# L1's self layers: transposing the attention weights head by head, and moving them in 4 KB pieces

## The chip, the cores and the metric

The kernel runs on one core of a Trainium2 chip, as one program. The metric is the time of one execution on the device in microseconds (us). The core has five engines with a queue of instructions each: TensorE (PE, matmuls; PEld is its loading of weights), VectorE (DVE), ScalarE (ACT), GpSimd (POOL) and SyncE (SP). Each runs its queue in order, and waits on semaphores for the others. DMAs are issued from SP's and POOL's queues here and run beside the engines.

## The reference

Four residual attention blocks follow one another on x (4 sequences of 1024 tokens, 256 channels, float32): L0 (self and cross attention, 16 heads, and a feed-forward part), L1 (three layers of 4 heads of 64 channels), L2 and L3 (16 heads, against a context of 77 tokens). The change is in L1, whose first layer attends to the context and whose second and third attend to their own tokens:

```python
Q = jax.nn.relu(q @ Wq + bq); K = jax.nn.relu(k @ Wk + bk); V = jax.nn.relu(v @ Wv + bv)
scores = jnp.einsum('hbqd,hbkd->hbqk', Qh, Kh) / jnp.sqrt(jnp.float32(dh))
scores = jnp.where(key_mask[None, :, None, :] == 0.0, NEG, scores)
attn = jax.nn.softmax(scores, axis=-1) * query_mask[None, :, :, None]
out = _layer_norm(jnp.einsum('hbqk,hbkd->hbqd', attn, Vh) + q, gamma, beta)
enc = jax.nn.leaky_relu(out @ Wff[i] + bff[i], negative_slope=0.2) + out
```

## The kernel before

All of x stays on the chip. A pipe (class Pipe) goes through the layers and, in each, through the four sequences. An item is one layer of one sequence. Its attention is cut into units; between the units the pipe's pump hands out steps of other work (projections of the next item, layer norm and output matmul of the one before) by costs that are written beside them. Only PE's order is the order of the text (manual_schedule); the queues of the other engines are ordered when the program is built, from what is ready, with the earlier instruction in the text first. `issue_after(ins)` adds that all instructions of a block on the engine of `ins` are queued behind `ins`; it adds no wait for its end.

In the self layers (class Self4) an item has 16 units: two pairs p of heads by eight tiles t of 128 query tokens. A unit does the following.

- Scores (L1262): for both heads h of the pair, PE multiplies 128 queries with all 1024 keys into a PSUM buffer `ss` of its own, [128, 1024]. There are two such buffers, so the next unit's scores of head h must wait until this unit's exponential of head h has read them.
- Maxima (L1273): VectorE reduces each `ss` to the negative maxima `nm`.
- Exponentials (L1279): ACT writes exp(ss + nm) into the buffer PR, and adds up the rows (`accum_out`). It permutes the columns as it writes: key number (k, c, i) of 8 x 4 x 32 goes to (c, k, i).
- The weights must be turned so that keys lie on the partitions. That is done by blocks: VectorE transposes each 32 x 32 block in place (L1291), and DMAs carry the blocks to other partitions of a buffer PT (L1298). A PR buffer holds a pair of units, t even and t odd; there are two, as of PT. The DMAs of a pair go out together: 16 of 128 KB, from 32 partitions (a) to 32 partitions (c).
- Weighted sums (L1334): PE multiplies the values V with PT, in two halves.
- `normal` (L1352 to L1364) turns the sums back, divides by the row sums and adds them to x.

The text puts these parts in different units. `scores` is called in unit u. `turned_by_blocks` is called in unit u + 1, behind the scores of that unit: it has the transpose of unit u, and, where t is odd, the pair's DMAs, SP and POOL taking turns with a. The halves of the weighted sums follow in units u + 3 and u + 4.

The lengths of the DMA pieces come from the layouts: PR is [128, 2 (t), 2 (h), 4 x 256], and a DMA takes 256 columns of each t and h, so its 32 partitions have four pieces of 1 KB each.

In the same queues stand, among others: on VectorE the statistics and scaling of the layer norm (L1536, L1583, L1586), its reciprocals and `normal`; on ACT all copies out of PSUM (L1512), the projections' Relu (L1233, L1194); on POOL the power of the variance (L1385); on SP the weights of the next layer (L1028, L1033), the bias rows cut into three parts (`thirds`, L2061) and the mask row of the keys (L1179). In the cross layer, L1501 and L1505 copy turned weights to a buffer PTc, on VectorE and ACT by turns.

## Time and profile before

| | us |
|---|---|
| median of 3 runs (2395.11 to 2406.44) | 2396.89 |
| the profiled execution, its own time | 2396.79 |
| its span, first to last instruction | 2394.9 |
| first to last unit of the self layers, from the span's start | 948 to 1880 |
| PE busy in the span | 2204.3 |
| VectorE busy | 1582.6 |
| ACT busy | 930.2 |
| POOL busy | 380.4 |

The page of the profile gives busy times, a row of 40 slices for each engine (a digit is the busy share in tenths), and groups of instructions: line, engine, operation, written and read buffers with their shapes, the number of instructions, then their busy time in us, the mean duration in ns, and the idle time of the engine just before them, with what ended most of it. The timeline gives start, duration, engine and line of single instructions, and in brackets an idle time before them with its end's cause. The granted clock is the share of its full clock that TensorE was given. A view of one buffer gives durations as least, median and greatest in ns.

### The profile page before, as it was taken

To read this page: it belongs to the slowest core of one execution; us is meant where nothing else is said; L and a number is where in the kernel's file an instruction comes from. 1 tells how busy PE (TensorE), PEld (TensorE's weight loads), DVE (VectorE), ACT (ScalarE), POOL (GpSimd) and SP (SyncE) were. 2 spreads that over 40 slices of the span, in tenths; PEclk is the share of its full clock that TensorE was granted. 3 is DMA by queue.
4 is the path that set the end of the run, shared out by engine and by line. 5 is a ranking of instruction groups with operands and counts; after the bars stand their busy time and mean duration, and the time that the engine had idled before them with its cause. 6 is when DMAs were issued, how large, how long until landed. Compare 5 with 4: busy or idle time off the path is not lost. (4 is left out here: it accounts for less than half of the span.)

```text
span 2394.9 us, 31195 instructions
## 1 busy us (share of the span) xinstructions
PE 2204.3 (92%) x11035; PEld 1204.8 (50%) x11035; DVE 1582.6 (66%) x3167; ACT 930.2 (39%) x1828; POOL 380.4 (16%) x648
## 2 busy tenths in 40 slices
PE   6899999999898979999999899999999899999996
PEld 3565446566577655545454445454545344444442
DVE  6665553534424565888888788888888656656765
ACT  2222332222232355545454454444444234434333
POOL 2000000000000000333333233333333100000000
PEclk8999989989998998999999999999999899999988
DMA  5000010000000000667776577766787400000000
GB/s 147 1 3 14 5 36 1 1 3 5 12 1 7 1 5 1 146 147 152 151 156 144 123 151 157 151 142 141 148 163 143 97 5 1 5 1 1 27 18 28
DMA packets 148677, 158.01 MB, mean 66 GB/s; under 512 B 51432, under 2 KB 130849, under 8 KB 148513
## 3 DMA queue, kind: packets, MB, share of 16 engines
q1 hardware_dynamic: 122161, 85.63, 17.2%
q0 software_dynamic: 25296, 69.24, 13.1%
q8 instruction: 91, 1.49, 0.3%
q10 hardware_dynamic: 1056, 1.05, 0.1%
q14 instruction: 73, 0.60, 0.1%
HBM read 17.41 MB, written 4.19 MB: 9 GB/s over the span
## 5 line engine op out<-in xcount | busy, mean ns | idle before, releaser
L1279 ACT ACTIVATE PR<-ss,nm 128x1024 f32<-128x1024 f32 x256 | 284.7, 1114 | 366.2 <-DVE nm L1273 290.2
L1291 DVE STREAM_TRANSPOSE PR<-PR 128x2048 f32<-128x2048 f32 x128 | 295.8, 2311 | 128.9 <-ACT PR L1279 114.3
L1298 POOL DMA_DIRECT2D PT<-PR x512 | 279.6, 554 | 577.7 <-PE ss L1262 236.7
L1262 PE MATMUL ss<-QK 64*128 64x512 f32 x1024 | 324.8, 628 | 28.8 <-ACT PR L1279 28.5
L1273 DVE TENSOR_REDUCE nm<-ss 128x1 f32<-128x1024 f32 x256 | 299.6, 1210 | 13.8 <-PE ss L1262 13.8
L377 ACT ACTIVATE PT<-pb 77x1024 f32<-77x1024 f32 x192 | 185.4, 1015 | 193.2 <-PE pb L373 193.2
L1334 PE MATMUL po<-PT,V 128*64 128x256 f32 x2048 | 251.1, 387 | 5.1 <-DMA PT<-PR 5.1
L281 DVE TENSOR_REDUCE mx<-pa 128x4 f32<-128x308 f32 x384 | 161.4, 470 | 83.7 <-PE pa L276 82.5
L1262 PEld LDWEIGHTS ss<-QK 64*128 64x128 f32 x1024 | 113.3, 187 | 176.8 <-ACT PR L1279 99.7
L1334 PEld LDWEIGHTS po<-PT,V 128*64 128x64 f32 x2048 | 136.6, 137 | 108.4 <-issue 51.1
L276 PE MATMUL pa<-KA,QT 64*128 64x308 f32 x768 | 169.1, 486 | 14.0 <-DVE mx L281 12.8
L1545 POOL TENSOR_TENSOR pw<-va,minus_half 128x4 f32<-128x4 f32 (+1 forms) x28 | 38.8, 1384 | 714.5 <-DVE va L1543 542.0
L386 PE MATMUL po<-PT,Vc 77*32 77x512 f32 x768 | 140.4, 639 | 7.6 <-ACT PT L377 7.0
L276 PEld LDWEIGHTS pa<-KA,QT 64*128 64x128 f32 x768 | 84.3, 193 | 99.1 <-issue 37.0
L604 PE MATMUL pp<-hF,w 128*128 128x256 f32 x512 | 116.9, 382 | 0.0
L367 PE MATMUL pb<-QT,KA 32*77 32x512 f32 x768 | 114.1, 665 | 0.0
L619 PE MATMUL pp<-w,hid 128*128 128x256 f32 x512 | 113.7, 379 | 0.0
L619 PEld LDWEIGHTS pp<-w,hid 128*128 128x128 f32 x512 | 97.0, 190 | 16.5 <-issue 2.2
L604 PEld LDWEIGHTS pp<-hF,w 128*128 128x128 f32 x512 | 95.6, 190 | 18.2 <-issue 6.0
L266 PE MATMUL pp<-hT,wq 128*128 128x512 f32 x192 | 98.0, 646 | 5.5 <-ACT hT L1507 5.0
L1536 DVE BATCH_NORM_STATS2 st<-x 128x6 f32<-128x256 f32 x256 | 97.7, 403 | 3.2 <-DMA x<-in_x 2.3
L1405 PE MATMUL pp<-wo,hE 128*128 128x256 f32 x384 | 96.4, 393 | 1.6 <-ACT hE L1512 1.6
(256 smaller groups left out, 3079.5 us busy)
## 6 DMA issues: line engine op xcount, KB each, us to landing
PT<-PR SPq DMA_DIRECT2D x512, 128.0 KB
PT<-PR POOLq DMA_DIRECT2D x512, 128.0 KB, 4.9
x<-in_x SPq DMA_DIRECT2D x4, 1024.0 KB
out<-x SPq DMA_DIRECT2D x8, 512.0 KB
w<-in_ff_w SPq DMA_DIRECT2D x2, 1024.0 KB
gb<-in_norms POOLq DMA_DIRECT2D x5, 256.0 KB, 6.6
wk<-in_l_wk SPq DMA_DIRECT2D x10, 128.0 KB
wv<-in_l_wv SPq DMA_DIRECT2D x5, 256.0 KB
```

The costliest lines, as they stand in the source:

```text
L276: nc.tensor.matmul(pas[i], self.qt[rows, e, ts(t, P)], self.ka[rows, e, :, :], start=True, stop=True)
L281: nc.vector.tensor_reduce(out, pas[i].rearrange("p (j s) k -> p j s k", s=2), AX.X, ALU.max, negate=True)
L377: nc.scalar.activation(pt[:, 2 * i : 2 * i + 2, :], pbs[i][:SC], AF.Exp, scale=self.l.scale)
L386: nc.tensor.matmul(po[ts(j, h.slot), :], l.v[:, self.b, col : col + h.vw], pt[:, j, :], start=True, stop=True)
L604: nc.tensor.matmul(pp[:, i, :], self.w1[:, cc, ts(f + i, P)], s["hT"][:, cc, ts(q, 2 * P)], start=cc == 0, stop=cc == NC - 1)
L619: nc.tensor.matmul(pp[:, u, :], s["a"][:, f, ts(u, P)], self.w2[:, f, :], start=f == 0, stop=f == NF - 1)
L1262: nc.tensor.matmul(ss[h][:, k, :], self.qk[p][rows, 0, ts(t, P)], self.qk[p][rows, 1, ts(k, 512)], start=True, stop=True,)
L1273: nc.vector.tensor_reduce(self.nm[:, t, at], s2, AX.X, ALU.max, negate=True)
L1279: nc.scalar.activation(out, s2, AF.Exp, bias=self.nm[:, t, at], accum_out=self.sums[:, t, at])
L1291: nc.vector.transpose(part, part)
L1298: (nc.sync, nc.gpsimd)[a % 2].dma_start(out=pt[ts(c, 32), :, :, a].rearrange("p t h k j -> p (t h) (k j)"), in_=pr[ts(a, 32), :, :, ts(c, ...
L1334: nc.tensor.matmul(po[64 * h : 64 * h + 64], self.v[:, k, 64 * (2 * p + h) : 64 * (2 * p + h) + 64], pts[:, :, h, :, k, :] if net.blocks e ...
```

## The change

The transposes move from `turned_by_blocks` into `scores`, into the unit whose weights they turn, and there are two of them, one for each head; both are queued behind the maxima of that unit's second head. `turned_by_blocks` is left with the DMAs and is called for odd t alone. PR is laid out as [128, 4 (c), 2 (t), 2 (h), 256], so that what one DMA takes from a partition is one piece of 4 KB; the exponential writes four pieces of 256 columns, 4 KB apart, where it wrote 1024 in a row, and a head's transpose works on such four pieces. PT has its dimension a ahead of t and h to match, so the written piece is of 4 KB too. SP issues the DMAs of a = 0, 1 and 2, POOL those of a = 3: twelve and four of a pair's sixteen. The weighted matmul reads the same 256 columns, in runs of 32, at other strides.

```diff
@@ scores @@
-            self.pr = net.tile("E", [P, 2, 2, S], name="PR")
+            self.pr = net.tile("E", [P, 4, 2, 2, S // 4], name="PR")
         for h in range(2):
             at = slice(2 * p + h, 2 * p + h + 1)
             s2 = ss[h].rearrange("p k n -> p (k n)")
-            nc.vector.tensor_reduce(self.nm[:, t, at], s2, AX.X, ALU.max, negate=True)
+            reduced = nc.vector.tensor_reduce(self.nm[:, t, at], s2, AX.X, ALU.max, negate=True)
             if net.blocks:
-                out = self.pr[:, t % 2, h, :].rearrange("p (c k i) -> p k c i", c=4, i=32)
+                out = self.pr[:, :, t % 2, h, :].rearrange("p c (k i) -> p k c i", i=32)
                 s2 = s2.rearrange("p (k c i) -> p k c i", c=4, i=32)
             else:
                 out = pr[:, h, :]
             nc.scalar.activation(out, s2, AF.Exp, bias=self.nm[:, t, at], accum_out=self.sums[:, t, at])
         if net.blocks:
-            net.pipe.later("next", 1, lambda pr=self.pr: self.turned_by_blocks(p, t, pr))
+            with net.tc.issue_after(reduced.ins):
+                for h in range(2):
+                    part = self.pr[:, :, t % 2, h, :]
+                    nc.vector.transpose(part, part)
+            if t % 2:
+                net.pipe.later("next", 1, lambda pr=self.pr: self.turned_by_blocks(p, t, pr))
@@ turned_by_blocks @@
-        part = pr[:, t % 2].rearrange("p h s -> p (h s)")
-        nc.vector.transpose(part, part)
-        if t % 2 == 0:
-            return
-
-        pt = net.tile("B", [P, 2, 2, 4, NT, 32], name="PT")
+        pt = net.tile("B", [P, 4, 2, 2, NT, 32], name="PT")
         for c in range(4):
             for a in range(4):
-                (nc.sync, nc.gpsimd)[a % 2].dma_start(
-                    out=pt[ts(c, 32), :, :, a].rearrange("p t h k j -> p (t h) (k j)"),
-                    in_=pr[ts(a, 32), :, :, ts(c, 256)].rearrange("p t h n -> p (t h) n"),
+                (nc.gpsimd if a == 3 else nc.sync).dma_start(
+                    out=pt[ts(c, 32), a].rearrange("p t h k j -> p (t h k j)"),
+                    in_=pr[ts(a, 32), c].rearrange("p t h n -> p (t h n)"),
                 )
@@ weighted @@
-                    pts[:, :, h, :, k, :] if net.blocks else pts[:, :, h, k, :], start=k == 0, stop=k == NT - 1,
+                    pts[:, :, :, h, k, :].rearrange("p a t j -> p t a j") if net.blocks else pts[:, :, h, k, :], start=k == 0, stop=k == NT - 1,
```

## The prediction

> **What bounds the kernel now.** The page comes first. The change touches only the self-attention of L1's second and third layer, where the lines L1262 to L1334 run; they fill the span from 948 to 1880 us.

> ```profile
> PE 2204.3 (92%) x11035; PEld 1204.8 (50%) x11035; DVE 1582.6 (66%) x3167; ACT 930.2 (39%) x1828; POOL 380.4 (16%) x648
> DVE  6665553534424565888888788888888656656765
> ...
> L1279 ACT ACTIVATE PR<-ss,nm 128x1024 f32<-128x1024 f32 x256 | 284.7, 1114 | 366.2 <-DVE nm L1273 290.2
> L1291 DVE STREAM_TRANSPOSE PR<-PR 128x2048 f32<-128x2048 f32 x128 | 295.8, 2311 | 128.9 <-ACT PR L1279 114.3
> ...
> L1273 DVE TENSOR_REDUCE nm<-ss 128x1 f32<-128x1024 f32 x256 | 299.6, 1210 | 13.8 <-PE ss L1262 13.8
> ```

> PE looks like the bound, but the idle columns say something else: in this stage VectorE sat idle 128.9 us ahead of its 128 transposes, 114.3 of them for ACT's exponentials, and only 13.8 us ahead of the maxima. So the scores are there before VectorE takes them. The timeline of one unit without other VectorE work shows the loop (start, duration, engine, line):

> ```profile
> 1314.81 2.31 DVE L1273 TENSOR_REDUCE nm<-ss 128x1 f32<-128x1024 f32 x2
> ...
> 1316.03 1.11 ACT L1279 ACTIVATE PR<-ss,nm 128x1024 f32<-128x1024 f32 x1 [2.91 <-DVE nm L1273]
> ...
> 1317.16 1.11 ACT L1279 ACTIVATE PR<-ss,nm 128x1024 f32<-128x1024 f32 x1
> ...
> 1317.28 3.11 PE L1262 MATMUL ss<-QK 64*128 64x512 f32 x8 [0.83 <-ACT PR L1279]
> 1318.17 0.19 ACT L1279 ACTIVATION_READ_ACCUMULATOR PR<-ss,nm 128x1 f32 x1
> ...
> 1318.39 2.31 DVE L1291 STREAM_TRANSPOSE PR<-PR 128x2048 f32<-128x2048 f32 x1 [1.27 <-ACT PR L1279]
> ...
> 1320.63 2.32 DVE L1273 TENSOR_REDUCE nm<-ss 128x1 f32<-128x1024 f32 x2
> ```

> Both maxima end at 1317.12; VectorE then idles 1.27 us until the second head's exponential and its accumulator read are done, transposes both heads in one instruction, and begins the next maxima 3.51 us after the last ones. PE pays for it: its score matmuls need the buffers that the exponentials free, so the eight take 3.11 us here, and 1.99 us where both buffers are free:

> ```profile
> 1204.00 1.99 PE L1262 MATMUL ss<-QK 64*128 64x512 f32 x8
> ```

> So the loop maxima, exponentials, transpose, maxima limits, with PE close behind. I went through the timeline for 126 units. In 124 the next maxima began because VectorE came free, not because scores came (the first head's scores had waited 1.6 us in the median unit). The wait inside the gap is over 1.1 us in 88 units, 0.3 to 1.1 in 21, less in 17, where layer-norm work filled it.

> **The change part by part.** (1) One transpose of 2048 becomes two of 1024. No row shows one. The reduces of 308 and 1024 elements (470 and 1210 ns, L281 and L1273) give 1.034 ns an element, so a transpose of 1024 takes 2311 less 1059, 1.25 us; two reduces in a row take 2.32 rather than 2.42, so I take 2.42 for the pair: 0.11 x 128 = 14 us more VectorE work. Ends: 2.31 (the second fixed cost hidden; the elements stay as many, so no less) and 2.71 (no overlap, and 0.1 for each because its pieces of 256 lie apart, as in part (5)), which is 51 us for the stage; 2.42 rests on the nearest rows.

> [...]

> (2) Head 0's transpose waits for the first exponential alone. In the unit above it could start at 1317.25 (0.02 after that accumulator read) and end at 1318.50; by then the second exponential is read out (1318.36), so the pair ends at 1319.67, not 1320.70. I take 0.98 us. The tie behind both maxima keeps them in the order they have now; behind the waiting transpose stand layer-norm and residual instructions, up to 3.1 us a unit, which ran after it before, too, in most units; PE waited for their results 0.8 us in all (L1396 behind L1364). Taking 0.98 where the wait is over 1.2, the wait less 0.25 elsewhere, VectorE gains 94 us over the stage; the extra 0.11 is in that. Ends: 0 (head 0 waits for both exponentials) and 129 (all idle time).

> (3) PE must follow. The excess over 1.99 us of the score matmuls, with PE's idle time before them, is 99 us, in 68 units. In the regular group 1526.41 to 1643.64 (16 units, 117.2 us) PE could do with 105.1. VectorE there has 37.5 maxima, 16 x 2.42 transposes, 22.2 other, and some 4 us of waits left: 102. Both floors lie near each other, but in different units, so neither is reached. I kept two running totals through the units: VectorE's lead grows by its gain, but not past the time by which that unit's scores had waited; PE's grows only where PE had waited. This gives 6.7 us in that group and 55 us in all. I take 50, as PE's waits for the copies of hT (8.7 us) and for thirds at layer changes (8.0) do not shrink. Ends: 0 and 99.

> (4) The DMAs. Sixteen of 128 KB a pair of units stay; pieces of 1 KB become 4 KB, and SP issues twelve, POOL four, where each had eight.

> ```profile
> L1298 SPq DMA_DIRECT2D PT<-PR x424: 585/801/1982, 1105.6 to 1874.6; - x142
> L1298 POOL DMA_DIRECT2D PT<-PR x424: 550/552/610, 1106.1 to 1871.6; - x142
> ```

> SP's eight take 8.0 us (0.6 each, then about 1.2 while both queues are full), POOL's 4.4; the last packets end 11.3 to 13.4 us after the transpose, and the weighted sums want them at 15 to 18. So nothing waits for them now. The DMA queues' shares (38.0% for 58.26 MB on SP's, 32.6% for 55.88 on POOL's, whose packets are 4 KB already) make large pieces about 10% cheaper a byte: 1 us a pair, hidden. Twelve issues at 0.6 to 0.85 us end at 7 to 10 us, so the landing stays near 12; with pairs 0.8 us shorter and transposes 1 us sooner it is wanted at 14.4 to 17. Cost 0. Weights, thirds and the mask row queue behind up to four more issues: at two layer changes at most 3 us each, within the ends. POOL's pow (L1385) comes 2 us sooner.

> [...]

> (5) The exponential writes runs of 32 at a longer stride, and the weighted matmul reads runs of 32 as before. L1279 (1114 ns) against the unpermuted L377 (1015) says one such permutation costs 0.1 us; this one is there already, so 0, at most 0.1 for each second exponential, 13 us. L1334's 387 ns equals L604's 382 with plain operands: 0.

> Sum: the profiled execution took 2396.79 us around a span of 2394.9, and the median of the runs is 2396.89, so both references agree. 2397 - 50 = 2347.

> **The rivals.** *PE or ACT takes over early.* ACT copies between exponentials move the second one out by up to 0.6 us (one at 1258.22), and VectorE's gain then ends in PE's own work. For it: PE is busy 89 to 98% of each 100 us, at a granted clock of 0.93 to 1.00; the regular group had 0.97, and at 0.93 PE's floor there would be 4.5 us higher, two thirds of the 6.7. Against it: the 99 us. Saving 10 to 25 us: about 2380.

> *Head 0 does not start early.* The heads now alternate in the buffer every 1 KB; if the dependency is taken over the whole stretch, the transpose waits for both exponentials: 128 x 0.11, 2411. Against it: the copies of PTc (L1501 and L1505) write alternate pieces from two engines, and those on ACT wait only for PE.

> *SP's queue sets the pace* (the slower side). Two pairs cannot be shorter than twelve issues, 3.5 us to the last landing, and some 12 us from a weighted sum to the end of the transpose two pairs on. At 1.0 us an issue a pair takes 13.75, the forecast; over 1.13 it is slower than the 14.53 of now (930 us by 64 pairs); at 1.2 for all twelve, 14.95 a pair, 64 x 0.42 = 27 more: 2424. For it: SP's 1.2 us issues. Against it: they come with POOL's traffic beside them, which halves.

> **How the numbers follow.** Forecast (2317 to 2372): 0.60. More than that: 0.06. Less, as in the first rival (2372 to 2409): 0.18, half of it beyond 0.5%. Head 0 held: 0.07. SP's pace: 0.09. A measurement here tells 0.5%, 12 us, from no change. Faster 0.60 + 0.06 + 0.09 = 0.75; same 0.09; slower 0.16. Range 2310 to 2409: it leaves out the slower cases and 0.04 below.

> **What would show it.** 256 transposes of 1024 near 1.25 us; VectorE's idle time before them under 40 us in place of 129, the first of each unit within 0.3 us of the maxima; score matmuls at 1.99 us in most units; SP issues under 0.9 us on the mean. It is wrong if the first transposes start only with the second exponential's end, or weighted sums wait for DMAs.

## The result, and the profile after

The changed kernel took 2413.41 us in the median of 20 runs (2399.74 to 2433.55), the kernel before 2401.68 beside it (20 runs, 2390.76 to 2411.99). The ratio is 1.0051, with a 95% interval of 1.0032 to 1.0069: slower by 0.5%, where 2347 was forecast. The profiled execution has a span of 2403.1 us, against 2394.9.

The lines of the page of the changed kernel that answer to those of before:

```profile
PE 2215.4 (92%) x11035; PEld 1216.6 (51%) x11035; DVE 1598.9 (67%) x3295; ACT 931.2 (39%) x1828; POOL 225.9 (9%) x392
...
L1279 ACT ACTIVATE PR<-ss,nm 128x1024 f32<-128x1024 f32 x256 | 284.0, 1113 | 248.7 <-DVE nm L1273 236.5
L1284 DVE STREAM_TRANSPOSE PR<-PR 128x1024 f32<-128x1024 f32 x256 | 305.6, 1225 | 87.1 <-ACT PR L1279 68.9
...
L1273 DVE TENSOR_REDUCE nm<-ss 128x1 f32<-128x1024 f32 x256 | 300.3, 1213 | 31.5 <-PE ss L1262 31.3
```

The 256 transposes are there, of 1225 ns each. VectorE's idle time ahead of them fell from 128.9 to 87.1 us only, and ACT is still what it waits for. ACT's idle time ahead of its exponentials fell too, from 366.2 to 248.7: ACT now waits somewhere else. Where, the list of ACT's waits between 1100 and 1880 us tells (engine, line, what it waited for, us in total, how often, the longest). Before:

```profile
ACT PR L1279 <- DVE nm L1273: 247.1, 82, 5.0
...
ACT hE L1512 <- PE pt L1396: 29.7, 12, 4.5
...
ACT V L1194 <- PE pv L1190: 9.7, 3, 6.9
...
ACT low L1410 <- PE pp L1405: 2.9, 2, 1.6
```

After:

```profile
ACT PR L1279 <- DVE nm L1273: 198.1, 56, 5.7
ACT V L1194 <- PE pv L1190: 41.9, 11, 6.1
ACT QK L1233 <- PE pp L1226: 35.6, 18, 3.5
ACT low L1411 <- PE pp L1406: 33.2, 14, 3.8
ACT QK L1233 <- PE pp L1231: 29.9, 13, 3.5
```

ACT's copies of the projections (V, QK, low) now wait for PE, some 140 us in all, where they waited 13 before. A copy that waits holds what is queued behind it. The timeline of one unit of the changed kernel shows what that is:

```profile
1541.24 1.99 PE L1262 MATMUL ss<-QK 64*128 64x512 f32 x8
1541.35 8.57 SPq L1299 DMA_DIRECT2D PT<-PR  x12
...
1543.15 3.70 PE L1226 MATMUL pp<-hT,wq 128*128 128x512 f32 x8
1543.26 2.36 DVE L1273 TENSOR_REDUCE nm<-ss 128x1 f32<-128x1024 f32 x2 [1.17 <-PE ss L1262]
...
1545.18 0.69 ACT L1233 ACTIVATE QK<-pp,qk_bias 128x512 f32<-128x512 f32 x1 [3.45 <-PE pp L1226]
...
1546.89 0.69 ACT L1233 ACTIVATE QK<-pp,qk_bias 128x512 f32<-128x512 f32 x1 [1.03 <-PE pp L1226]
1547.48 1.11 ACT L1279 ACTIVATE PR<-ss,nm 128x1024 f32<-128x1024 f32 x1
...
1548.71 2.37 DVE L1284 STREAM_TRANSPOSE PR<-PR 128x1024 f32<-128x1024 f32 x2 [3.10 <-ACT PR L1279]
```

The first maximum is done at about 1544.5, but the first exponential starts at 1547.48: two QK copies stand ahead of it, and they wait for projections that PE runs behind this unit's own scores. VectorE then idles 3.10 us, more than the 1.27 of the unit shown before. I summed the delay of each unit's first exponential behind its maximum over 126 units (the second to the 127th): 12.5 us before, 118.7 after. In the next unit (1549.25) the two transposes do what was forecast: the first starts 0.32 us behind the maxima and the pair ends 2.67 us behind them, where it took 3.58 in the unit shown before.

The DMAs of the changed kernel, by the view of the buffer PT:

```profile
L1299 SPq DMA_DIRECT2D PT<-PR x768: 507/590/2190, 963.3 to 1907.0; - x192
L1299 POOL DMA_DIRECT2D PT<-PR x256: 489/489/580, 963.5 to 1900.3; - x128
```

SP's median issue is 590 ns, where it was 806 over the whole run before, and twelve take 8.57 us in the unit above. The weighted sums wait no longer for DMAs than before: PE idles once ahead of them, for the last pair of the stage, 5.4 us where it was 5.1.

So ACT's queue has another order. In the built programs one can count what stands on ACT between the exponentials of two successive units: in the kernel before, 10 of 127 gaps are empty and 17 hold five or more instructions; in the changed kernel 51 are empty, and 39 hold five to eight, in bunches, ahead of a first exponential. Which part of the change did that was the question of the experiments. It is not the tie: without `issue_after` the built program is the same, instruction by instruction.

### The profile page after: what moved, and what is told of

Its sections match the earlier page's. It is cut to its first block, busy times and chain, and to the rows that moved or that the text cites. A ratio compares the mean times of both kernels' runs of the same rounds, so it can differ in the third digit from the quotient of the medians.

```text
span 2403.1 us, 30934 instructions
## 1 busy us (share of the span) xinstructions
PE 2215.4 (92%) x11035; PEld 1216.6 (51%) x11035; DVE 1598.9 (67%) x3295; ACT 931.2 (39%) x1828; POOL 225.9 (9%) x392
## 5 line engine op out<-in xcount | busy, mean ns | idle before, releaser
L1279 ACT ACTIVATE PR<-ss,nm 128x1024 f32<-128x1024 f32 x256 | 284.0, 1113 | 248.7 <-DVE nm L1273 236.5
L1284 DVE STREAM_TRANSPOSE PR<-PR 128x1024 f32<-128x1024 f32 x256 | 305.6, 1225 | 87.1 <-ACT PR L1279 68.9
L1262 PE MATMUL ss<-QK 64*128 64x512 f32 x1024 | 338.5, 634 | 22.5 <-ACT PR L1279 21.3
L1273 DVE TENSOR_REDUCE nm<-ss 128x1 f32<-128x1024 f32 x256 | 300.3, 1213 | 31.5 <-PE ss L1262 31.3
L1335 PE MATMUL po<-PT,V 128*64 128x256 f32 x2048 | 257.5, 395 | 5.4 <-DMA wk<-in_l_wk 5.4
L377 ACT ACTIVATE PT<-pb 77x1024 f32<-77x1024 f32 x192 | 185.2, 1014 | 192.5 <-PE pb L373 192.5
L281 DVE TENSOR_REDUCE mx<-pa 128x4 f32<-128x308 f32 x384 | 161.8, 471 | 80.5 <-PE pa L276 79.6
L1262 PEld LDWEIGHTS ss<-QK 64*128 64x128 f32 x1024 | 124.6, 190 | 174.6 <-ACT PR L1279 90.2
L1299 POOL DMA_DIRECT2D PT<-PR x256 | 124.8, 494 | 778.7 <-DVE st L1537 172.6
L1335 PEld LDWEIGHTS po<-PT,V 128*64 128x64 f32 x2048 | 138.8, 139 | 111.4 <-issue 55.4
L604 PE MATMUL pp<-hF,w 128*128 128x256 f32 x512 | 116.9, 382 | 0.0
L604 PEld LDWEIGHTS pp<-hF,w 128*128 128x128 f32 x512 | 95.6, 190 | 18.2 <-issue 6.0
```

The lines of the kernel that those rows point to most:

```text
L281: nc.vector.tensor_reduce(out, pas[i].rearrange("p (j s) k -> p j s k", s=2), AX.X, ALU.max, negate=True)
L377: nc.scalar.activation(pt[:, 2 * i : 2 * i + 2, :], pbs[i][:SC], AF.Exp, scale=self.l.scale)
L604: nc.tensor.matmul(pp[:, i, :], self.w1[:, cc, ts(f + i, P)], s["hT"][:, cc, ts(q, 2 * P)], start=cc == 0, stop=cc == NC - 1)
L1262: nc.tensor.matmul(ss[h][:, k, :], self.qk[p][rows, 0, ts(t, P)], self.qk[p][rows, 1, ts(k, 512)], start=True, stop=True,)
L1273: reduced = nc.vector.tensor_reduce(self.nm[:, t, at], s2, AX.X, ALU.max, negate=True)
L1279: nc.scalar.activation(out, s2, AF.Exp, bias=self.nm[:, t, at], accum_out=self.sums[:, t, at])
```

## The experiments

The theory: PE, VectorE and the split are as forecast, and the order of ACT's queue, which the program's builder derived anew, took the gain. Rivals: PE is the bound and nothing was to be had; SP's twelve issues cost time on the chip; splitting costs; VectorE's order does it. Each experiment ran beside the kernel before on the same chip, and its ratio is to that.

**e1_queues_8_8**

```diff
-                (nc.gpsimd if a == 3 else nc.sync).dma_start(
+                (nc.sync, nc.gpsimd)[a % 2].dma_start(
```

> The change, with the DMAs of a pair issued by SP and POOL in turns, eight and eight, as before; split and tied transposes and 4 KB pieces stay. In the built program ACT's queue is then in nearly the order of before (2 to 3 copies between the exponentials of two units, 5 of 127 gaps empty), where in the changed kernel 51 of 127 gaps are empty and 5 to 8 copies come in one bunch. Theory (twelve issues on SP made the builder reorder ACT's queue; the first exponential then stands behind copies that wait for PE): ratio to before 0.975 to 0.985, the delay of exponential 0 behind its maximum falls from 119 us in all to under 25. Rival 1 (nothing is to be gained, because PE becomes the bound as soon as VectorE is quicker): 0.995 to 1.005. Rival 2 (splitting or moving the transposes itself costs): 1.00 to 1.01, as the changed kernel.

Measured: 0.9727 (0.9700 to 0.9753), 2332.12 us, a little better than the theory's range; the delay is 8.5 us. One line of the change undone turns a loss of 0.5% into a gain of 2.7%. The same unit in this kernel:

```profile
1479.89 7.01 SPq L1299 DMA_DIRECT2D PT<-PR  x7
...
1480.51 3.70 PE L1226 MATMUL pp<-hT,wq 128*128 128x512 f32 x8
...
1480.69 2.35 DVE L1273 TENSOR_REDUCE nm<-ss 128x1 f32<-128x1024 f32 x2
...
1481.94 1.11 ACT L1279 ACTIVATE PR<-ss,nm 128x1024 f32<-128x1024 f32 x1 [2.46 <-DVE nm L1273]
...
1483.18 2.38 DVE L1284 STREAM_TRANSPOSE PR<-PR 128x1024 f32<-128x1024 f32 x2
...
1484.18 1.26 ACT L1233 ACTIVATE QK<-pp,qk_bias 128x512 f32<-128x512 f32 x2
```

The same two QK copies come behind both exponentials; VectorE goes from maxima to transposes in 0.14 us. Its page answers to that of the changed kernel:

```profile
L1284 DVE STREAM_TRANSPOSE PR<-PR 128x1024 f32<-128x1024 f32 x256 | 307.7, 1229 | 23.4 <-ACT PR L1279 14.6
L1273 DVE TENSOR_REDUCE nm<-ss 128x1 f32<-128x1024 f32 x256 | 300.9, 1216 | 32.0 <-PE ss L1262 30.9
```

**e2_before_12_4**, the kernel before with the opposite edit:

```diff
-                (nc.sync, nc.gpsimd)[a % 2].dma_start(
+                (nc.gpsimd if a == 3 else nc.sync).dma_start(
```

> The kernel before with one edit: SP issues twelve and POOL four of a pair's sixteen DMAs; layout, 1 KB pieces and the one transpose stay. Theory (the builder reorders ACT's queue because of the queues alone): ACT's queue has the bunches of the changed kernel (51 of 127 gaps empty), the delay of exponential 0 rises from 12 us to about 100 us in all, and the time rises to 1.015 to 1.03 of before, since no gain of the split pays for it. Rival 1 (PE is the bound, ACT's order matters little): within 0.5% of before. Rival 2 (the split costs, not the queues): within 0.5% of before. Rival 3 (SP's queue on the chip sets the pace with twelve issues of 1 KB pieces, 1.2 us each): also over 1.015, but then weighted sums wait for the DMAs.

Measured: 1.0203 (1.0174 to 1.0232). The queues alone, with no transpose touched, cost 2%, and ACT's waits are those of the changed kernel:

```profile
ACT V L1194 <- PE pv L1190: 49.5, 12, 6.4
ACT QK L1233 <- PE pp L1231: 35.9, 13, 4.0
ACT QK L1233 <- PE pp L1226: 34.8, 18, 3.4
```

PE's only wait ahead of a weighted sum is the one at the end of the stage (5.6 us, 5.1 in the kernel before), which speaks against the third rival, but the queues and the order still come together in this run.

**e4_split_alone**, the kernel before with the moved and split transposes; `turned_by_blocks` keeps its DMAs and is called for odd t alone:

```diff
...
+            with net.tc.issue_after(reduced.ins):
+                for h in range(2):
+                    part = self.pr[:, t % 2, h, :]
+                    nc.vector.transpose(part, part)
...
```

> Of the change only the split and moved transposes with their tie; the layouts, the 1 KB pieces and the eight and eight DMAs of before. ACT's queue is in the same order as with the change at eight and eight. Theory: as e1, 0.975 to 0.985 of before, within 0.5% of e1, since the pieces are hidden. Rival (pieces of 4 KB matter): over 0.5% above e1. Rival (splitting costs): 1.00 to 1.01.

Measured: 0.9747 (0.9717 to 0.9777). The intervals of e1 and e4 overlap: pieces of 4 KB bring nothing that shows, and the whole gain belongs to the transposes, which are both moved and split here. The next run parts the two.

**e8_moved_unsplit**

```diff
-                for h in range(2):
-                    part = self.pr[:, :, t % 2, h, :]
-                    nc.vector.transpose(part, part)
+                part = self.pr[:, :, t % 2]
+                nc.vector.transpose(part, part)
```

> e1_queues_8_8 with one transpose for both heads, still in the unit whose weights it turns and behind both maxima. It tells the split from the move. By the prediction's step 2 the gain is that of head 0 starting early, so this should be within 0.7% of before (0.993 to 1.005), VectorE idle again over 1 us before the transposes of most units. Rival (the move alone, by the order that the builder makes of it, brings the gain): under 0.985.

Measured: 1.0002 (0.9977 to 1.0028). Moved but not split, nothing is gained, and VectorE's idle time is that of before (last columns). ACT's order is not quite that of e1 here (10 empty gaps in place of 5), but the delay of the first exponentials, 14.1 us in place of 8.5, leaves little to it:

```profile
L1283 DVE STREAM_TRANSPOSE PR<-PR 128x2048 f32<-128x2048 f32 x128 | 295.8, 2311 | 129.7 <-ACT PR L1279 120.4
```

**Orders and queues apart.** In the next four, PINS lists the instructions of one or two engines, from the first to the last maximum or exponential of the self layers, in the order that another kernel's build gave them, and each is tied behind the one ahead of it. The ties only order; they add no wait. The queues of SP and POOL are left to the builder.

```diff
+    def pin(self):
+        traced = {i.name: i for i in self.nc.cur_bb.bb.instructions}
+        for names in PINS:
...
+            for a, b in zip(names, names[1:]):
+                self.tc.add_manual_dep(
+                    traced[b], a,
+                    mybir.DependencyInfo(mybir.DependencyClass.NoSync, mybir.DependencyReason.DATA), reason="issue_after",
+                )
```

**e5_act_order**: the changed kernel, ACT in the order of e1.

> The changed kernel, twelve and four DMAs and all, whose ACT instructions from the first to the last exponential of the self layers are tied into exactly the order of e1_queues_8_8; the ties add no wait. VectorE's order stays, but for some places, that of the changed kernel. Theory (ACT's order alone took the gain): 0.970 to 0.985 of before. Rival 1 (twelve issues on SP cost on the chip itself, beside any order): 1.00 to 1.01. Rival 2 (VectorE's order, which the queues changed too, does it): over 0.99.

Measured: 0.9806 (0.9771 to 0.9841).

**e6_act_dve_order**: the changed kernel, ACT and VectorE in the order of e1.

> As e5_act_order, and VectorE's instructions of the same stretch are tied into the order of e1_queues_8_8 as well, so that only the queues that issue the DMAs differ from e1. Theory (orders, not queues): within 0.5% of e1, 0.968 to 0.978 of before. Rival 1 (the queues cost on the chip): 1.00 to 1.01. If e5 stays at the changed kernel's time and this one falls, it was VectorE's order.

Measured: 0.9772 (0.9734 to 0.9809).

**e7_8_8_bad_order**: e1, ACT and VectorE in the order of the changed kernel.

> The opposite of e6: e1_queues_8_8 with its DMAs issued by SP and POOL in turns, eight and eight, and ACT's and VectorE's instructions tied into the order of the changed kernel. Theory: as slow as the changed kernel, 1.00 to 1.012 of before. Rival 1 (the queues cost on the chip): 0.97 to 0.98, as e1.

Measured: 1.0152 (1.0117 to 1.0187), slower still than the theory's range.

**e11_dve_order**: the changed kernel, VectorE in the order of e1.

> The changed kernel with VectorE's instructions of the self layers tied into the order of e1_queues_8_8; ACT's order stays that of the changed kernel but for some places (46 empty gaps in place of 51). Theory (ACT's order is the cause): 0.995 to 1.007 of before. Rival (VectorE's order does it): under 0.985.

Measured: 1.0054 (1.0030 to 1.0079).

With the changed kernel and e1 these make a square:

| | orders of e1 | orders of the changed kernel |
|---|---|---|
| eight and eight | 0.9727 (e1) | 1.0152 (e7) |
| twelve and four | 0.9772 (e6) | 1.0051 (the change) |

The time follows the column. Down the first column the queues differ by 0.45%, and the intervals overlap; down the second, twelve and four is even the quicker by 1%. So SP's twelve issues cost nothing in the regular units that can be told on the chip. The 0.45% is 11 us. Of PE's waits for an exponential one is 13.0 us long in e6 (the last number), where e1's longest is 1.8; it could be all of the 11:

```profile
PE ss L1372 <- ACT PR L1389: 20.9, 19, 13.0
```

It stands at a change of layers (1288.51 to 1301.52). VectorE, in e1's order, turns there to a bias row and waits 13.3 us for its load, which SP issues only at 1296.53, behind a run of the DMAs into PT; in e1 SP had issued it at 1263.91. SP's order was not tied, so whether the wait comes of that order or of the longer queue is open.

ACT's order alone (e5) takes the change from 1.0051 to 0.9806, 59 us of 2400; VectorE's alone (e11) brings nothing, though e11 has the same wait, of 12.9 us, so that some 0.5% may hide in it. From e5 to e6 the intervals overlap; what VectorE's order adds on top is open. Why e7 is slower than the changed kernel wasn't tried; its trace has VectorE waiting 12.3 us for POOL's power (14 times) where the changed kernel has 0.9.

**e12_queues_10_6**

```diff
-                (nc.gpsimd if a == 3 else nc.sync).dma_start(
+                (nc.gpsimd if (4 * c + a) % 8 in (1, 4, 6) else nc.sync).dma_start(
```

> The changed kernel with ten of a pair's sixteen DMAs on SP and six on POOL. In built programs the empty gaps between two units' exponentials on ACT number 5 of 127 at eight and eight, 3 at nine, 32 at ten, 43 at eleven, 51 at twelve. Theory (the bunches cost, in proportion): the delay of exponential 0 between e1's 8.5 and the changed kernel's 118.7 us, about 60 to 80, and the time about half way, 0.985 to 0.998 of before. Rival (a few places in ACT's order matter, not the bunches): as e1, under 0.978, or as the changed kernel, over 1.002.

Measured: 0.9837 (0.9795 to 0.9879), with a delay of 72.2 us. Between the two, as the theory has it, a little better than forecast. In built programs with all twelve on POOL and four on SP there are 51 empty gaps too, and 61 with all sixteen on either: the length of the longer queue decides, not whose it is. That the builder takes a queue's issues for a bound that they are not on the chip fits this, but its rule was not looked into.

**e3_act_tied**: the obvious mend, a tie that keeps the copies behind the exponentials.

```diff
-        if scores:
-            scores()
-        self.call("next")
...
+        tie = scores() if scores else None
+        with tie[0].issue_after(tie[1]) if tie else nullcontext():
+            self.call("next")
...
+            return net.tc, exp.ins
```

> The changed kernel, with twelve and four DMAs, and one tie more: what a self-layer unit traces behind its scores is queued on ACT behind that unit's second exponential, so that no copy of the unit's projections can stand ahead of its exponentials. Theory (ACT's order took the gain): delay of exponential 0 near 0, ratio to before 0.975 to 0.99; copies come later than now for PE, which may take back some of it. Rival (SP's twelve issues cost on the chip itself, by their queue): 1.00 to 1.01, as the changed kernel. Rival (PE is the bound): 0.995 to 1.005.

Measured: 1.0181 (1.0151 to 1.0212), outside the ranges of the theory and of both rivals. The delay of the first exponential was 11.8 us as wanted, and VectorE idled 18.3 us ahead of the transposes; the time was lost elsewhere. PE's waits from 950 to 1880 us:

```profile
PE pm L1175 <- DVE neg L1158: 43.6, 7, 10.5
PE pt L1168 <- ACT hT L1515: 29.5, 6, 5.0
```

The tie also held back the row sums xs of the next item, from which VectorE makes the mask row, and the copies of hT. I took the sums for the main loss.

**e9_act_tied_but_sums**: the same tie without the sums.

```diff
+        for i in traced[at:]:
+            if i.engine == tie[1].engine and i.name not in self.free:
+                tie[0].add_manual_dep(
...
```

> As e3_act_tied (the changed kernel, twelve and four, the rest of a unit queued on ACT behind its second exponential), except for the row sums xs (L1162) that the mask of the next item needs, which stay free. In e3 PE waited 43.6 us for that mask row (L1175 behind L1158) and 29.5 us for copies of hT. Theory (twelve issues are harmless once ACT's exponentials go first, and e3 lost by the sums that it held back): 0.972 to 0.985 of before, and PE's wait for the mask row is gone. Rival (e3 lost because copies behind the exponentials come late for PE in general, so ACT's order cannot be had by such a tie): 1.00 to 1.02, as e3.

Measured: 0.9971 (0.9949 to 0.9993), between the ranges of the theory and of the rival. The mask row is waited for no more, and the time is 2.1% below e3's; the copies of hT remain (PE's waits from 940 to 1900 us):

```profile
PE pt L1176 <- ACT hT L1523: 30.2, 6, 5.0
```

**e10_8_8_tied**: this tie on e1.

> The same tie on e1_queues_8_8, as a version that might beat it: no copy between the exponentials of a unit (28 in e1), 2 empty gaps in place of 5. Theory: e1's delay of exponential 0 was 8.5 us and of exponential 1 13.3 us in all, so at most 20 us are left in it: 0.965 to 0.975. Rival (copies that come later delay PE as much): 0.973 to 0.985.

Measured: 0.9784 (0.9753 to 0.9815), in the rival's range: not better than e1. PE waited 14.1 us for hT, against 4.8 in e1, where those copies may stand between exponentials. So the tie is too blunt, and e1 is the best version found. ACT's order is the same in e9 and e10 but for some places (589 of 605 agree in the built programs), VectorE's is not (600 of 1115 from the first to the last maximum), and the two differ by 1.9%. The granted clock is part of it (window, its length, busy times, then the clock, the DMA share and GB/s), e9 first:

```profile
948.90:1865.00 916.10, 861.10 (x4265) 433.71 (x4264) 790.80 (x1114) 443.31 (x903) 146.14 (x275) 0.96 0.60 148
```

```profile
945.80:1825.20 879.40, 852.34 (x4265) 428.74 (x4264) 788.88 (x1115) 441.86 (x903) 263.89 (x527) 0.98 0.68 154
```

What of the 36.7 us between them is VectorE's order and what the later hT is not settled.

All runs in one table. Delay: of the first exponentials, in 126 units. Idle: VectorE's, ahead of the transposes. PE: excess of the score matmuls over 1.99 us with PE's idle time ahead of them, in the same units.

| | ratio | delay | idle | PE |
|---|---|---|---|---|
| before | 1 | 12.5 | 128.9 | 97.5 |
| the change | 1.0051 | 118.7 | 87.1 | 105.3 |
| e1 | 0.9727 | 8.5 | 23.4 | 45.5 |
| e2 | 1.0203 | 111.4 | 172.2 | 133.2 |
| e3 | 1.0181 | 11.8 | 18.3 | 50.9 |
| e4 | 0.9747 | 7.3 | 22.2 | 44.3 |
| e5 | 0.9806 | 15.6 | 29.5 | 50.4 |
| e6 | 0.9772 | 13.0 | 27.3 | 58.7 |
| e7 | 1.0152 | 125.1 | 92.6 | 115.3 |
| e8 | 1.0002 | 14.1 | 129.7 | 97.5 |
| e9 | 0.9971 | 12.2 | 16.0 | 59.9 |
| e10 | 0.9784 | 6.7 | 15.3 | 48.1 |
| e11 | 1.0054 | 105.0 | 115.7 | 126.8 |
| e12 | 0.9837 | 72.2 | 65.0 | 70.7 |

## Why the prediction was wrong

The step that failed is (4), "Cost 0". It priced the twelve and four DMAs by what they do to the queues on the chip, and there it was right but for one wait (e6). But the orders of all queues except PE's are made anew when the program is built, and a longer DMA queue changes ACT's. Part (2) leaned on the same gap: it looked at what stands behind the waiting transposes on VectorE and took the ACT instructions for fixed. The section on the kernel before says how the orders arise, and no step drew on it. In place of the 0 the runs show a cost of 59 us by e5, 67 with VectorE's order (1.0051 less 0.9772), larger than the whole gain of 50: the first exponentials start 118.7 us late in all, for 12.5 before, behind copies on ACT that wait for PE.

Step by step, with e1, which is the change as the steps saw it:

1. Two transposes for one. They are 1225 to 1229 ns each and 2.36 to 2.38 for the pair; 1.25 and 2.42 were forecast. (By its own rows the pair comes to 2.40: twice 1.25 less the 0.10 that two reduces save.) The added busy time is 307.7 less 295.8, 11.9 us, for 14 forecast. Two transposes back to back cost 0.06 us a unit more than the one of before (2.37, in the changed kernel's unit above, less 2.31). By the single durations it would be 0.15 (twice the 1.229 of e1, less 2.311); back to back, part of that overlaps.
2. Head 0 starts early. VectorE's idle time fell by 105.5 us in e1; less the 11.9, that is 93.6, where 94 was forecast. e8 shows that neither the move nor the pieces of 4 KB give it.
3. PE follows. Its excess and waits fell from 97.5 to 45.5, by 52, where the account gave 55 and 50 was taken. In the regular group 16 units take 107.3 us in e1 (1477.61 to 1584.95) for 117.2 before: 9.9, where 6.7 was forecast. The measured gain, 2.7% or 66 us, is above the 50; the profiled executions differ by 72.4, some of it ahead of the self layers (first unit at 934.7 for 948.2, at a granted clock of 0.97 for 0.95; e4, at 947.1 and 0.95, does not share it). From the first scores to the last transpose the stage took 930.6 us before, 871.8 in e1 and 868.4 in e4: 59 to 62 us less.
4. On the chip nothing waits for the twelve in the changed kernel, as said; in e6 PE waits once 13 us by way of a bias row behind them, where at most 3 us at a change of layers were allowed for. With pieces of 4 KB SP's queue takes about 8% less of the DMA engines' time than with pieces of 1 KB by e1 and e4 (16.2% of a span of 2322.5 us, 17.6% of 2334.3; see the last section), where about 10% was forecast, and it hides. On the order, see above.
5. Strides cost nothing: exponentials 1113 to 1115 ns, weighted matmuls 387 before and 389 in e1.

Two rivals lay on the slower side, and neither mechanism is what happened. "Head 0 does not start early" gave 2411, next to the 2413, by luck: the first transposes start 0.32 us behind the maxima in the median unit, and in e1, with the same layout, VectorE's wait is down to 23.4 us. "SP's queue sets the pace" gave 2424: SP issues at 0.6 to 0.7 us, and e6 runs at 0.9772 with twelve of them. "ACT takes over early" named ACT's copies, yet only those between two exponentials, at 10 to 25 us.

## What to carry to other kernels

Where a builder orders the queues, a change has two costs: what it does on the chip in today's order, and what order it makes. Count, before trusting a forecast, whether the other engines' queues still stand in the order that the trace shows; here one line about DMA queues moved ACT's copies ahead of its exponentials. A copy that waits for the engine it feeds, queued ahead of the instruction on the critical loop, is the sign to look for, and a tie that holds back everything is no safe mend for it.

## What the runs showed of the hardware

A wait of PE can cost more than its length. In the changed kernel PE idles from 1284.46 to 1286.57 us, and a little later its granted clock (third column from the end) is half:

```profile
1281.00:1284.00 3.00, 3.00 (x22) 2.11 (x22) 2.84 (x3) 1.48 (x5) 1.05 (x3) 1.00 0.94 242
1284.46:1286.57 2.11, 0.00 (x0) 0.00 (x0) 0.28 (x2) 1.75 (x5) 0.00 (x0) 1.00 0.89 280
1287.60:1293.60 6.00, 6.00 (x10) 2.35 (x10) 4.71 (x6) 2.47 (x6) 0.00 (x0) 0.50 0.29 65
```

Four projection matmuls of L1226 take 3.40 us from 1291.38, at a mean clock of 0.57, and 1.98 us from 1171.55, at 1.00.

e3, with twelve waits of 5 us and longer, has a mean clock of 0.94 in the stage where e1 has 0.99. That the idle time is the cause is read from the sequence; no run took it by itself. The window need not be idle throughout: PE was busy for 38% of the one at 1284.0 in the changed kernel, and the next was at 0.50.

Pieces of 4 KB for 1 KB make the same 85.63 MB of SP's queue take 16.2% in place of 17.6% of the DMA engines' time (e1 and e4), which hides here.
